# An attention and expert layer on one core: PSUM banks by name, and side work queued behind the score copies and adds

## The chip, the cores and the metric

The kernel runs on one core of one Trainium2 chip. The metric is the device time of an execution in microseconds (us), and of several executions the median. The time before is 2626.7 us (three runs, 2624.99 to 2631.52).

## The reference

The input x has 4096 rows (2 sequences of 2048) of 2048 numbers. Each row is normalised, and the normalised rows xn go through single-head attention with head width 512 and through a mixture of 64 small experts of rank 8; both results are added to x. All of it is fp32.

```
xn   = layernorm(x)
qkv  = xn @ Wqkv + bqkv            # q, k, v: 4096 x 512 each
attn = softmax(q k^T / sqrt(512))  # per sequence, 2048 x 2048
x   += (attn @ v) @ Wo + bo
gate = softmax over the 16 largest of 64 router scores, else 0
x   += ((xn @ A^T) * gate per group of 8) @ B^T * 2
```

## The kernel before

**Numbers and products.** TensorE multiplies in a rounded fp32 form. Each operand is split into a rounded part (ScalarE, `split_hi`, line 121) and the rest (VectorE, `split_lo`, line 124), and every product takes three matmuls (`PASSES`: rest x rounded, rounded x rest, rounded x rounded). The large products are also done on 2 x 2 block matrices with seven block products in place of eight. The seven steps are called P1 to P7, and they need sums of operands and sums of results.

**Stages.** From 0 to about 1321 us rows are normalised and projected: a first block of 512 rows (`first_block`), a second one, and then three pairs of blocks, each in seven phases P1, P2, P6, P5, P3, P7, P4 (`phase`). Side work (loads, splits, sums) is listed per phase in `beside` and dealt out between the pieces of a phase. From 1321 to 2015 us comes attention, then the output projection to the end.

**Attention.** Queries are taken in four pairs of 512-row blocks, `NPAIR` = 4, eight blocks in all. For each pair there are `NKS` = 8 key groups of seven score steps, 56 steps a pair, 224 in all. A score step (`score`) is six matmuls (line 1129) from a query operand `qt` and a key operand `kt`. Steps P1, P7, P2, P6, P4, P5, P3 follow each other, and P1 of the next group is put before P3. In a group, P1 and P2 add up in one PSUM bank, P7 and P4 in a second, and P6, P5, P3 in a third, called U, which first gets a copy of P1 (`seed`, line 1112, on ScalarE). Results leave as copies on ScalarE (lines 1142, 1144, 1147, 1155) or as adds on VectorE (lines 1149, 1152) into the score tiles `sp`, and running maxima M are kept (lines 1098, 1101).

When a block's scores are there, `maxes` reduces the maxima to one per query (a chain of small VectorE instructions that ends in `mq`, line 1176), and `spread` brings them to all partitions with one matmul (line 1186) and a ScalarE copy. `soft` subtracts them (line 1201), takes the exponential (line 1204), splits (tile `ph`) and adds up row sums L (lines 1212, 1214). `weigh` multiplies by the values: a block has 16 key tiles of four columns d of 128 output features, so 64 groups of three matmuls (line 129, tile `ph` by `vt`), which add up over the block in four banks `av`. Near the end of a block two matmuls (lines 1248, 1249) sum L over partitions, VectorE takes the reciprocal `rl` (line 1251), and after the last column the four divisions follow (line 1255), each with a bias on ScalarE (line 1256) and a store to DRAM (line 1257). The tiles `ot` have three buffers.

The value products of a pair run beside the scores of the next one, dealt evenly between `begin[i]` and `begin[i + 1]`. The last 9 of the 233 steps and the last pair have no scores beside them.

**Side work of attention.** The dictionary `side` holds steps by score number: key blocks split and stored for later pairs (`keys`: loads `kr`, casts and sums into `kst`, stores to `kp_d`), query operands (`query_load`, `query_split`), sums of queries (`query_steps`: four loads, four sums at lines 928 to 931, four stores, for each of two halves), and sums of output weights (`combos`).

**What sets the order.** A list scheduler orders the instructions of each engine when the kernel is built; each engine then runs its own queue in that order. `behind(keys)` adds an edge that keeps what is traced under it after a given instruction on the same engine. Under it, side steps of attention are kept behind the last key load on SyncE's queue:

```
for st in side.get(g, []):
    with behind("sp"):
        st()
```

[...] One, `misc`, is for small things. The other seven are one pool of seven buffers, from which the scheduler gives any free one:

```
def acc():
    return psum.tile([P, T], F32, name="acc", tag="acc", bufs=7)
```

Of the kernel before, what the change touches and what calls it, by code (L numbers as in the profile page):

```python
# [8 lines left out]
F32 = mybir.dt.float32  # L9
FR = mybir.dt.float32r  # L10
AF = mybir.ActivationFunctionType
# [5 lines left out]
P = 128  # L17
# [45 lines left out]
def attn_ffn_kernel(ctx: ExitStack, tc, x, xT, wq, wv, wob, bqk, bv, bo, keysT, out):  # L63
# [17 lines left out]
    def big(*js):  # L81
        return Ring(sb, *(f"B{j}" for j in js))
# [12 lines left out]
    for tag, words in order:  # L95
        sb.tile([P, words], F32, name=f"slot{tag}", tag=tag, bufs=1)

    def acc():
        return psum.tile([P, T], F32, name="acc", tag="acc", bufs=7)

    def misc(shape=None):
        return psum.tile(shape or [P, T], F32, name="misc", tag="misc", bufs=1)
# [49 lines left out]
    def oz_at(i, kind, c):  # L152
        return oz_d[i][c // 2, 2 * kind + c % 2]
# [507 lines left out]
    def beside(j, ph):  # L661
# [33 lines left out]
        if ph == "P3":  # L695
            if more:
                n = x_steps(j + 1, *b00)
                steps = mixed(split_steps(j, "P7", *b01), n[1][:2])
                return n[0], s1[-2:-1] + steps[:3] + s1[-1:] + steps[3:]
            return [], mixed(  # L700
                split_steps(j, "P7", *b01), query_steps(0, big(*GROUPS[3]), (0,))
            )
        if ph == "P7":
            if more:
                n = x_steps(j + 1, *b10)
                return n[0], mixed(split_steps(j, "P4", *b10), n[1][:2])
            ks_ = key_list(5, 7)
            return [], mixed(
                split_steps(j, "P4", *b10), query_steps(0, big(*GROUPS[3]), (1,)), ks_[:-4]
            ) + ks_[-4:]  # L710
        if more:
            return x_steps(j + 1, *b01)[0] + x_steps(j + 1, *b11)[0], mixed(
# [199 lines left out]
            steps += ops  # L912
        return steps

    def query_steps(j, ring, ds=(0, 1)):

        def steps(d):
            v = {}
            tt = nc.vector.tensor_tensor

            def load():
                for h in range(2):
                    for t in range(2):
                        v[h, t] = ring([P, T], F32, "qs")
                        nc.sync.dma_start(v[h, t], q_d[2 * j + t][h][:, d, :])

            def sums():
                tt(v[1, 1], v[1, 1], v[0, 1], ALU.subtract)
                tt(v[0, 1], v[0, 1], v[0, 0], ALU.subtract)
                tt(v[0, 0], v[1, 1], v[0, 0], ALU.add)  # L930
                tt(v[1, 0], v[1, 0], v[0, 0], ALU.subtract)

            def out():
                for k, at in enumerate(((0, 1), (0, 0), (1, 1), (1, 0))):
                    nc.sync.dma_start(qs_d[j][k][:, d, :], v[at])

            return [load, sums, out]

        return [st for d in ds for st in steps(d)]

    def query_load(j, n, ring=None):

# [163 lines left out]

    def seed(k):

        b = bank["U"] = acc()
        if k < 3:  # L1110
            nc.tensor.matmul(b, bank["k"], bank["q"], start=True, stop=True)
        nc.scalar.copy(b, bank["P1"])  # L1112

    def score(g):

# [5 lines left out]
            bank["U0"] = bank["U"]  # L1121
        name = {"P2": "P1", "P4": "P7", "P6": "U0", "P5": "U0", "P3": "U0"}.get(step, step)
        if not more:
            bank[step] = acc()
        ps = bank[name]
        st, mv = kop.pop(g), qop[j, step]
        for d in range(2):
            for i, (a, c) in enumerate(PASSES):
# [2 lines left out]
                    start=not more and d == 0 and i == 0, stop=d == 1 and i == 2,  # L1131
                    skip_group_check=more,
                )
        tt, copy = nc.vector.tensor_tensor, nc.scalar.copy
        if later:
            greatest(*later.pop())
        if step == "P1":
# [92 lines left out]
    def weigh(n):  # L1230

        c, d = divmod(n, ND)
        blk, k = blocks[c // NK], c % NK
        if d == 0:
            load_v(c + 3)
            soft(c + 2)
        if k == 0:
            av[blk, d] = acc()
        vt, ph = vt_[c], pt_[c]
        product(  # L1240
            av[blk, d], lambda a: vt[:, a, d * P : (d + 1) * P], lambda b: ph[:, b, :],
            k == 0, k == NK - 1,
        )
        if k == NK - 2 and d == 2:
            lh, ll = lsum[blk]
            with behind("pe"):
                pl = misc()
                nc.tensor.matmul(pl, onesr, ll, start=True, stop=False)
                nc.tensor.matmul(pl, onesr, lh, start=False, stop=True)
            rl_[blk] = r_rl([P, T], F32, "rl")  # L1250
            nc.vector.reciprocal(rl_[blk], pl)  # L1251
        if k == NK - 1 and d == ND - 1:
            for d in range(ND):
                ot = r_oo([P, T], F32, "ot")
                nc.vector.tensor_tensor(ot, av[blk, d], rl_[blk], ALU.mult)  # L1255
                nc.scalar.activation(ot, ot, AF.Identity, bias=bv_sb[:, d : d + 1])
                nc.sync.dma_start(oz_at(blk, 1, d), ot)

# [200 lines left out]
    NW = 2 * NK * ND  # L1461
    total = NPAIR * NG1

    begin = [NG1 * (j + 1) + (9 if j in (0, NPAIR - 1) else 5) for j in range(NPAIR)]
    side = {}

    def deal(g, steps, every=1):
# [18 lines left out]
        ks.update(R=mid(0, 1), st=mid(2, 3), n=1)  # L1486

    r_qs = wide(3, 4, 5, 9)
    for g, st in zip((2, 6, 8, 12, 16, 18), query_steps(1, r_qs)):
        deal(g, [st])  # L1490
    deal(NG1 + 2, [small_ring])
    for n, g in (
        (11, NG1 + 6), (12, NG1 + 18), (13, NG1 + 48), (14, 2 * NG1 + 9), (15, 2 * NG1 + 19)
# [23 lines left out]
    deal(begin[0] - 8, [lambda c=c: load_v(c) for c in range(3)])  # L1517
    deal(begin[0] - 3, [lambda c=c: soft(c) for c in range(2)])
    done = 0
    for g in range(begin[-1]):  # L1520
        if g < total:
            score(g)
# [1 line left out]
                key_load(g // 2 + 4)  # L1524
        j, n = divmod(g, NG1)
        for st in side.get(g, []):
            with behind("sp"):
                st()
        if j and j <= NPAIR:
            if n == 2:  # L1530
                maxes(2 * j - 1)
            if n in (1, 4):
                with behind("pe"):
                    spread(2 * j - 2 + n // 4)
        if n == NG1 - 2 and j < NPAIR:
            maxes(2 * j)
        for i in range(NPAIR - 1):
# [117 lines left out]
```

## Time and profile before

| | us |
|---|---|
| median of three runs (lowest, highest) | 2626.7 (2624.99, 2631.52) |
| profiled execution, its own time | 2629.96 |
| span of its instructions | 2628.2 |
| TensorE busy in matmuls | 2592.6 (99%) |
| VectorE busy | 1919.4 (73%) |
| ScalarE busy | 909.8 (35%) |
| GpSimd busy | 516.1 (20%) |

The profile is of one execution. An engine is busy while one of its instructions runs. Matmuls are pipelined and their ends are modelled, so a matmul has a mean of 389 ns though the next starts 227 ns after it. PE is TensorE's matmul side and PEld its weight loads, DVE is VectorE, ACT is ScalarE, POOL is GpSimd, SP is SyncE, whose queue issues nearly all DMAs. In a row of waits the columns are: the engine and line that waited, who released it, us in total, times, and the longest. In a row of a tile's instructions they are: least, median and largest ns, then first and last start. In a timeline row they are: start, us, engine, line, what it does, and in brackets the idle time before it and what ended that.

### The profile page before, as it was taken

Reading aid. Unit: us, or ns where it says so; the run is one execution under the profiler, and the core shown is the slowest. Engines: PE = TensorE matmul, PEld = TensorE weight load, DVE = VectorE, ACT = ScalarE, POOL = GpSimd, SP = SyncE. Lnnn points to the kernel's source line nnn. Section 1 sums busy time; section 2 is a strip of 40 time slices with the busy share of each in tenths; the row PEclk is TensorE's granted clock in tenths of the full one; section 3 lists DMA queues with packets and bytes.
Section 4 is the critical chain, followed back from the end, with each engine's and each line's share of the span. In section 5 each row is a group of like instructions: output and inputs, shape, how many; then the busy total and the mean of one; then the engine's idle time right before and its main releaser. Section 6 shows DMA issues by size and latency. Waiting matters only on the chain. (4 is left out here: it accounts for less than half of the span.)

```text
span 2628.2 us, 34501 instructions
## 1 busy us (share of the span) xinstructions
PE 2592.6 (99%) x12692; PEld 2186.3 (83%) x12692; DVE 1919.4 (73%) x2698; ACT 909.8 (35%) x1345; POOL 516.1 (20%) x315
## 2 busy tenths in 40 slices
PE   8999999999999999999989999999999999999999
PEld 7889888888888888888877877878888888888887
DVE  7557639867878677776758859678598776797675
ACT  4323223323332333343435436344364222332221
POOL 1311420000000000000000000000000765566654
PEclk9999999999999999999999999999999999999999
DMA  6667875668447683576999798799788544565542
GB/s 235 232 248 261 284 262 186 211 211 278 153 136 226 214 274 124 177 257 226 310 305 326 253 329 268 257 331 321 251 294 296 175 164 161 183 217 176 177 162 103
DMA packets 328954, 608.09 MB, mean 231 GB/s; under 512 B 27928, under 2 KB 150864, under 8 KB 328784
## 3 DMA queue, kind: packets, MB, share of 16 engines
q1 hardware_dynamic: 315824, 575.99, 64.9%
q10 hardware_dynamic: 12960, 29.89, 3.4%
q8 instruction: 100, 1.64, 0.3%
q14 instruction: 70, 0.57, 0.1%
HBM read 450.42 MB, written 155.35 MB: 230 GB/s over the span
## 5 line engine op out<-in xcount | busy, mean ns | idle before, releaser
L129 PE MATMUL acc<-t,pw 128*128 128x512 f32 x3024 | 694.0, 390 | 1.6 <-DVE pw L124 1.5
L129 PEld LDWEIGHTS acc<-t,pw 128*128 128x128 f32 x3024 | 565.3, 188 | 119.7 <-DVE pw L124 2.5
L1406 PE MATMUL acc<-wb,s 128*128 128x512 f32 x2688 | 609.4, 389 | 0.0
L1406 PEld LDWEIGHTS acc<-wb,s 128*128 128x128 f32 x2688 | 504.5, 188 | 104.8
L1390 POOL TENSOR_TENSOR xo<-xo,bo_bc 128x512 f32<-128x512 f32 x128 | 205.6, 1613 | 906.4 <-DMA vt<-v_d 606.2
L129 PE MATMUL acc<-ph,vt 128*128 128x512 f32 x1536 | 378.6, 391 | 4.5 <-DVE ot L1255 2.5
L1129 PE MATMUL acc<-qt,kt 128*128 128x512 f32 x1344 | 338.4, 394 | 14.3 <-ACT acc L1112 7.4
L129 PEld LDWEIGHTS acc<-ph,vt 128*128 128x128 f32 x1536 | 287.7, 188 | 68.5 <-DVE ot L1255 4.1
L1129 PEld LDWEIGHTS acc<-qt,kt 128*128 128x128 f32 x1344 | 253.1, 190 | 73.7 <-ACT acc L1112 8.3
L121 ACT CAST pw<-pw 128x1024 fp32r<-128x1024 f32 (+1 forms) x168 | 177.6, 1058 | 324.8 <-PE acc L129 240.9
L129 PE MATMUL acc<-xh,wh 128*128 128x512 f32 x1152 | 263.7, 390 | 0.0
L124 DVE TENSOR_TENSOR pw<-pw 128x1024 fp32r<-128x1024 f32 (+1 forms) x168 | 214.7, 1278 | 64.9 <-ACT pw L121 63.5
L129 PEld LDWEIGHTS acc<-xh,wh 128*128 128x128 f32 x1152 | 215.6, 188 | 44.9
L129 PEld LDWEIGHTS acc<-pw,t 128*128 128x128 f32 x2016 | 245.8, 188 | 1.3
L129 PE MATMUL acc<-pw,t 128*128 128x264 f32 x2016 | 246.4, 283 | 0.0
L121 ACT CAST s<-xz 128x1024 fp32r<-128x1024 f32 x112 | 118.0, 1054 | 368.7 <-PE acc L1406 285.8
L124 DVE TENSOR_TENSOR s<-xz,s 128x1024 fp32r<-128x1024 f32 x112 | 175.4, 1568 | 41.6 <-ACT s L121 41.6
L124 DVE TENSOR_TENSOR wh<-wu,wh 128x512 fp32r<-128x512 f32 x96 | 83.6, 888 | 99.0 <-ACT wh L121 99.0
L519 POOL TENSOR_TENSOR zt<-zt,g 128x512 f32<-128x512 f32 x24 | 38.9, 1630 | 503.3 <-DMA g<-gd 272.4
L121 ACT CAST t<-xq 128x1024 fp32r<-128x1024 f32 x84 | 88.3, 1052 | 103.5 <-PE acc L129 44.8
L124 DVE TENSOR_TENSOR t<-xq,t 128x1024 fp32r<-128x1024 f32 x84 | 108.2, 1292 | 20.6 <-ACT t L121 20.1
L1395 DVE TENSOR_TENSOR xo<-xo,acc 128x512 f32<-128x512 f32 x128 | 86.8, 679 | 49.1 <-PE acc L1406 22.3
(168 smaller groups left out, 2463.2 us busy)
## 6 DMA issues: line engine op xcount, KB each, us to landing
vt<-v_d SPq DMA_DIRECT2D x128, 512.0 KB, 5.3
kt<-kp_d SPq DMA_DIRECT2D x224, 256.0 KB, 5.8
pw<-sq_d SPq DMA_DIRECT2D x72, 512.0 KB, 4.0
xo<-in_x SPq DMA_DIRECT2D x128, 256.0 KB, 3.4
xz<-oz_d SPq DMA_DIRECT2D x64, 512.0 KB, 4.8
out_y<-xo SPq DMA_DIRECT2D x128, 256.0 KB, 2.3
pw<-in_wq SPq DMA_DIRECT2D x54, 512.0 KB, 4.4
wu<-in_wq SPq DMA_DIRECT2D x48, 512.0 KB, 5.9
```

Of the source, the lines that this page charges most:

```text
L121: return nc.scalar.copy(hi, src)
L124: return (eng or nc.vector).tensor_tensor(lo, src, raw(hi), ALU.subtract)
L129: last["pe"] = nc.tensor.matmul(ps, st(a_), mv(b_), start=first and n == 0, stop=end and n == 2)
L519: nc.gpsimd.tensor_tensor(zt, zt, gx[n], ALU.mult)
L1129: last["pe"] = nc.tensor.matmul(ps, st[:, d, a, :], mv[c][:, d, :], start=not more and d == 0 and i == 0, stop=d == 1 and i == 2, skip_gro ...
L1390: nc.gpsimd.tensor_tensor(xs, xs, bo_bc[q // (NB // 2 * NH), c], ALU.add)
L1395: nc.vector.tensor_tensor(xs, xs, ps, op)
L1406: nc.tensor.matmul(ps, st[a_][:, kk, sl], mv[b_], start=not more and kk == 0 and n == 0, stop=kk == ND - 1 and n == 2, skip_group_check=more,)
```

## The change

1. `acc()` gives banks by name, from 0 to 6. Without an argument the seven names go round. In attention the names are fixed: the four value columns have banks 0 to 3, P1/P2 has bank 4, U bank 5, P7/P4 bank 6. In the odd key groups of the first pair, when no value products run yet, P1, U and P7 have banks 0, 1 and 2.
2. A side step of attention is kept behind the last score copy on ScalarE and the last score add on VectorE too, besides the last key load.
3. The query sums of pair 1 leave attention for projection phase P7 of the last pair, and those of pair 0, which were half in P3 and half in P7, are all in P3.
4. The division of a column follows the last product of that column, not that of the fourth column.
5. The second maxima and both spreads come one score step later (steps 3, 2, 5 of a pair, not 2, 1, 4), and the value products of the middle pairs begin one step later.
6. One of three dummy matmuls in `seed` goes.

```diff
@@ -95,8 +95,14 @@
     for tag, words in order:
         sb.tile([P, words], F32, name=f"slot{tag}", tag=tag, bufs=1)
 
-    def acc():
-        return psum.tile([P, T], F32, name="acc", tag="acc", bufs=7)
+    banks = list(range(7))
+
+    def acc(n=None):
+
+        if n is None:
+            n = banks.pop(0)
+            banks.append(n)
+        return psum.tile([P, T], F32, name="acc", tag=f"acc{n}", bufs=1)
 
     def misc(shape=None):
         return psum.tile(shape or [P, T], F32, name="misc", tag="misc", bufs=1)
@@ -698,7 +704,7 @@
                 steps = mixed(split_steps(j, "P7", *b01), n[1][:2])
                 return n[0], s1[-2:-1] + steps[:3] + s1[-1:] + steps[3:]
             return [], mixed(
-                split_steps(j, "P7", *b01), query_steps(0, big(*GROUPS[3]), (0,))
+                split_steps(j, "P7", *b01), query_steps(0, big(*GROUPS[3]))
             )
         if ph == "P7":
             if more:
@@ -706,7 +712,7 @@
                 return n[0], mixed(split_steps(j, "P4", *b10), n[1][:2])
             ks_ = key_list(5, 7)
             return [], mixed(
-                split_steps(j, "P4", *b10), query_steps(0, big(*GROUPS[3]), (1,)), ks_[:-4]
+                split_steps(j, "P4", *b10), query_steps(1, big(*GROUPS[2])), ks_[:-4]
             ) + ks_[-4:]
         if more:
             return x_steps(j + 1, *b01)[0] + x_steps(j + 1, *b11)[0], mixed(
@@ -912,7 +918,7 @@
             steps += ops
         return steps
 
-    def query_steps(j, ring, ds=(0, 1)):
+    def query_steps(j, ring):
 
         def steps(d):
             v = {}
@@ -936,7 +942,7 @@
 
             return [load, sums, out]
 
-        return [st for d in ds for st in steps(d)]
+        return steps(0) + steps(1)
 
     def query_load(j, n, ring=None):
 
@@ -1106,10 +1112,10 @@
 
     def seed(k):
 
-        b = bank["U"] = acc()
-        if k < 3:
+        b = bank["U"] = acc(5 - 4 * (k < NKS and k % 2))
+        if k < 2:
             nc.tensor.matmul(b, bank["k"], bank["q"], start=True, stop=True)
-        nc.scalar.copy(b, bank["P1"])
+        last["copy"] = nc.scalar.copy(b, bank["P1"])
 
     def score(g):
 
@@ -1121,7 +1127,7 @@
             bank["U0"] = bank["U"]
         name = {"P2": "P1", "P4": "P7", "P6": "U0", "P5": "U0", "P3": "U0"}.get(step, step)
         if not more:
-            bank[step] = acc()
+            bank[step] = acc((4 if step == "P1" else 6) - 4 * (k < NKS and k % 2))
         ps = bank[name]
         st, mv = kop.pop(g), qop[j, step]
         for d in range(2):
@@ -1131,7 +1137,13 @@
                     start=not more and d == 0 and i == 0, stop=d == 1 and i == 2,
                     skip_group_check=more,
                 )
-        tt, copy = nc.vector.tensor_tensor, nc.scalar.copy
+
+        def tt(*ops):
+            last["add"] = nc.vector.tensor_tensor(*ops)
+
+        def copy(*ops):
+            last["copy"] = nc.scalar.copy(*ops)
+
         if later:
             greatest(*later.pop())
         if step == "P1":
@@ -1235,7 +1247,7 @@
             load_v(c + 3)
             soft(c + 2)
         if k == 0:
-            av[blk, d] = acc()
+            av[blk, d] = acc(d)
         vt, ph = vt_[c], pt_[c]
         product(
             av[blk, d], lambda a: vt[:, a, d * P : (d + 1) * P], lambda b: ph[:, b, :],
@@ -1249,12 +1261,11 @@
                 nc.tensor.matmul(pl, onesr, lh, start=False, stop=True)
             rl_[blk] = r_rl([P, T], F32, "rl")
             nc.vector.reciprocal(rl_[blk], pl)
-        if k == NK - 1 and d == ND - 1:
-            for d in range(ND):
-                ot = r_oo([P, T], F32, "ot")
-                nc.vector.tensor_tensor(ot, av[blk, d], rl_[blk], ALU.mult)
-                nc.scalar.activation(ot, ot, AF.Identity, bias=bv_sb[:, d : d + 1])
-                nc.sync.dma_start(oz_at(blk, 1, d), ot)
+        if k == NK - 1:
+            ot = r_oo([P, T], F32, "ot")
+            nc.vector.tensor_tensor(ot, av[blk, d], rl_[blk], ALU.mult)
+            nc.scalar.activation(ot, ot, AF.Identity, bias=bv_sb[:, d : d + 1])
+            nc.sync.dma_start(oz_at(blk, 1, d), ot)
 
 
 
@@ -1461,7 +1472,7 @@
     NW = 2 * NK * ND
     total = NPAIR * NG1
 
-    begin = [NG1 * (j + 1) + (9 if j in (0, NPAIR - 1) else 5) for j in range(NPAIR)]
+    begin = [NG1 * (j + 1) + (9 if j in (0, NPAIR - 1) else 6) for j in range(NPAIR)]
     side = {}
 
     def deal(g, steps, every=1):
@@ -1486,8 +1497,6 @@
         ks.update(R=mid(0, 1), st=mid(2, 3), n=1)
 
     r_qs = wide(3, 4, 5, 9)
-    for g, st in zip((2, 6, 8, 12, 16, 18), query_steps(1, r_qs)):
-        deal(g, [st])
     deal(NG1 + 2, [small_ring])
     for n, g in (
         (11, NG1 + 6), (12, NG1 + 18), (13, NG1 + 48), (14, 2 * NG1 + 9), (15, 2 * NG1 + 19)
@@ -1517,6 +1526,7 @@
     deal(begin[0] - 8, [lambda c=c: load_v(c) for c in range(3)])
     deal(begin[0] - 3, [lambda c=c: soft(c) for c in range(2)])
     done = 0
+    last["add"] = last["dve"]
     for g in range(begin[-1]):
         if g < total:
             score(g)
@@ -1524,14 +1534,14 @@
                 key_load(g // 2 + 4)
         j, n = divmod(g, NG1)
         for st in side.get(g, []):
-            with behind("sp"):
+            with behind("sp", "copy", "add"):
                 st()
         if j and j <= NPAIR:
-            if n == 2:
+            if n == 3:
                 maxes(2 * j - 1)
-            if n in (1, 4):
+            if n in (2, 5):
                 with behind("pe"):
-                    spread(2 * j - 2 + n // 4)
+                    spread(2 * j - 2 + n // 5)
         if n == NG1 - 2 and j < NPAIR:
             maxes(2 * j)
         for i in range(NPAIR - 1):
```

## The prediction

> **What bounds the kernel now.** I read the page's busy table first, then stretches by stage, then TensorE's waits in the attention stage, then the start times of single matmuls around each wait.
>
> ```profile
> PE 2592.6 (99%) x12692; PEld 2186.3 (83%) x12692; DVE 1919.4 (73%) x2698; ACT 909.8 (35%) x1345; POOL 516.1 (20%) x315
> L1406 PE MATMUL acc<-wb,s 128*128 128x512 f32 x2688 | 609.4, 389 | 0.0
> ```
> TensorE is the bound, with little to give: in the output projection 2688 matmuls take 609.4 us, 226.7 ns each, with no idle time. That is the floor for any 512-column matmul here.
>
> ```profile
> 0.00:1321.00 1321.00, 1310.07 (x7098) 1136.09 (x7099) 942.68 (x1476) 445.18 (x686) 146.74 (x91) 1.00 0.67 226
> 1321.00:2015.00 694.00, 673.24 (x2909) 545.99 (x2909) 534.11 (x802) 314.46 (x493) 9.94 (x7) 0.99 0.87 295
> 2015.00:2628.00 613.00, 609.32 (x2689) 504.20 (x2687) 442.56 (x421) 150.14 (x167) 359.40 (x217) 1.00 0.52 172
> ```
> After the stretch: its length, then busy us of PE, PEld, DVE, ACT, POOL, the clock and the DMA share. The attention stage, 694 us, holds some 2907 matmuls, at 226.7 ns 659 us: 35 us are lost. The busy column shows only 21 of them, because ends of matmuls are modelled. So only attention has something to win.
>
> ```profile
> PE acc L1129 <- ACT acc L1112: 7.4, 2, 7.2
> PE acc L1129 <- ACT sp L1155: 5.0, 5, 1.6
> PE acc L129 <- DVE ot L1255: 2.5, 2, 2.2
> PE acc L1129 <- DMA kt<-kp_d: 1.9, 3, 0.8
> PE misc L1186 <- DVE mq L1176: 1.8, 3, 1.0
> PE acc L129 <- DVE ph L124: 1.7, 2, 1.2
> ```
> Adding up, from the starts, what each interval has over 0.227 us, 33.9 us fall to: stage start 9.9, late score copies 7.4, maxima with their spreads (L1186) 5.4, key loads 3.1, block ends (division, softmax) 8.0. The start is ScalarE's queue:
>
> ```profile
> 1323.63 0.41 ACT L121 CAST kst<-kr 128x256 fp32r<-128x256 f32 x1 [9.56 <-DMA kr<-k_d]
> 1329.69 1.06 ACT L121 CAST vs<-vs 128x264 fp32r<-128x264 f32 x3 [0.32 <-DVE vs L289]
> 1330.65 0.57 ACT L1112 COPY acc<-acc 128x512 f32<-128x512 f32 x1
> ```
> Six casts of a key block, waiting for a load, stand ahead of the first seed copy, with the value casts behind them; the copy is all that TensorE lacks, and it stops from 1323.9 to 1331.3. At 1620.2 it is the same in small: key casts that wait for their stores stand ahead of an L1155 copy, and TensorE loses 1.8 us. The next 11 matmuls then start 0.427 us apart, not 0.227.
>
> ```profile
> L1251 DVE RECIPROCAL rl<-misc x8: 3339/3348/3358, 1500.9 to 2011.6; 128x512 f32<-128x512 f32 x8
> L1255 DVE TENSOR_TENSOR ot<-acc,rl x32: 671/678/693, 1505.9 to 2022.1; 128x512 f32<-128x512 f32 x32
> L1256 ACT ACTIVATE ot<-ot,bv_sb x32: 705/722/727, 1506.6 to 2022.8; 128x512 f32<-128x512 f32 x32
> DMA to landing us min/median/max: 2.2/3.5/6.0
> ```
> The chain at a block's end (the last line is its stores) matters below.
>
> [...] a stop of 2.4 us at 1511.6 was followed by 1.6 us of such loss and one of 2.4 us at 38.6 by none. [...] divisions at 1972.4 come only after the reciprocal of 1968.6 to 1971.9. [...] a new holder waits for the old one's reader, as at 1511.6 for the division.
>
> **The change part by part.** Where instructions land I take from the built order of each engine; counts are equal but for one dummy matmul less (-0.2 us).
>
> Side work behind copies and adds. The first seed copy now has three value casts ahead and no key cast; later, key casts alternate with copies. But the names put the first score in bank 4, held by the last value tile: two adds L289 (0.42 each) and hops, about 0.9 us, and some 0.3 for bank 6. Start: 9.9 becomes 1.2 (0.8 to 4). **-8.7.**
>
> Late copies. Before, P7 of the next key group took the bank that P3's copy (L1155) frees, one step earlier: six product matmuls, 1.36 us, to hide 0.59 plus the queue. Now P7 has bank 6, freed three steps before; P3's copy is wanted only by the next seed copy, and that by P2: 18 matmuls, 4.1 us, against 1.5 for both copies. The worst lateness seen (1.6 beyond 0.8) fits. 7.4 becomes 1.6 (0 to 5). **-5.8.** What the change pushes back, casts and sums for keys, queries and weights, is used steps later.
>
> Query sums. Pair 1's 8 sums (0.68 each), 8 loads and 8 stores (256 KB, 4.2 MB) leave 1321 to 1421, where the DMA share is 0.96. They go to phase P7 (1234 to 1278, share 0.83), and half of pair 0's from there to P3 (0.75). DVE is busy 33 and 28 of 44 us there, so 2.7 us more each are covered; 2.1 MB more in 44 us is 48 GB/s on 281, close to full. On SP they pass weight fetches, issued over a piece of 24 matmuls (5.4 us) ahead: +0.3 (0 to 3). Key loads: 3.1 becomes 1.6 (0 to 3). **-1.2.**
>
> Maxima later. One score step and its products, about 2.5 us, cover the worst mq wait (1.16); some 0.3 per spread stays, 8 times. 5.4 becomes 2.4 (2 to 4). **-3.0.**
>
> Division per column and named product banks. There are eight block ends; I number them 1 to 8, and the last three (6, 7, 8) come when all scores are done. A new block's column d now waits for the old one's division d; before, it could take any free bank, and without scores three were free. (At end 8 the next holder of bank 0 is the output projection's first sum.) From the second L1249 matmul to the end of the first division the trace has 6.1, 9.7, 5.3, 12.7, 7.4, 6.3, 7.1, 6.2 us (VectorE's queue over the bare 3.35 + 0.68). The new VectorE order adds a softmax cast and a maximum at ends 2 and 3 (1.2), takes about 2 from end 4, and a stop at end 6 lets VectorE gain about 1.8 for end 7: 6.1, 10.9, 6.6, 10.5, 7.4, 6.3, 5.3, 6.2. TensorE asks after 6.4, 8.1, 7.7, 9.0, 6.4 us (27 to 39 matmuls), but after 3.65 (15) at the three ends without scores: stops of 0, 2.8, 0, 1.5, 1.0, 2.6, 1.6, 2.5, together 12.0. The fourth division needs the first one's buffer back (0.72 + 3.5 + 0.68 and hops, 5.1 us) and TensorE comes after 17 matmuls (3.9) at end 6 and some 20 (4.5) at ends 1 and 2: 2.3. Half clock after the three long stops: 1.6 each, at even odds 2.4. Sum 16.7 (5 to 40) instead of 8.0: **+8.7.**
>
> First block. Naming puts the last transposes of row tile 1 into the bank of the first accumulator, so the statistics of tile 2 (2.46 us) start 2 us later; but TensorE waited 2.4 us anyway for those of tile 3, which come 0.4 later: **+0.4** (0 to 3). Projection and output order is otherwise the same.
>
> Sum: -8.7 - 5.8 - 1.2 - 3.0 + 8.7 + 0.4 - 0.2 = -9.8. The profiled execution took 2629.96 us (span 2628.2) and would take 2620.2; the median of the runs, 2626.7, is 3.3 lower: 2617.
>
> **The rivals.** (a) Slower: the ends decide. Where the reciprocal's chain is never absorbed, each of eight ends costs 3.5 us (the mean over the three without scores, with the fourth column) and 1.6 of half clock, 41 in all: 33 - 18.5 = +14.5, 2641. It needs over 26.5 us in all, 3.3 per end; 4.3 per end is 0.3%. For it: DVE is busy without a break from 1957 to 1975. Against: ends 1 and 3 have chains of 6.1 and 5.3 under TensorE's 6.4 and 7.7. (b) No change: copies stay late (5 of 7.4) and ends cost 21: 2625. For it: exponentials of 1.06 us still stand between P3's copy and the seed. (c) Everything hides: VectorE, relieved early, keeps ahead and ends cost 5: 2605. For it: the last reciprocal waited 1.8 us idle; against: nothing shortens 3.35.
>
> **How the numbers follow.** A measurement tells 0.3% (7.9 us) from no change. My forecast 0.40 and (c) 0.17 are faster; (b) and the weak side of my forecast 0.26; (a) 0.17. The range, 2603 to 2635, leaves about 0.1 out on each side; it takes in the bounds of the start, the copies and the loads, and most of (a).
>
> **What would show it.** Right: no key cast ahead of the first L1112; hardly any wait of L1129 on L1155; TensorE's longest stops at the last three block ends, on ot. Wrong: new waits on ACT or kt in the first pair, stops on pw near 1234 to 1278, or none at all at the ends.

## The result, and the profile after

The changed kernel takes **2638.36 us** (median of 20 runs, 2631.35 to 2643.02); beside it on the same chip the kernel before takes 2630.85 (20 runs). The ratio is 1.0029, 95% interval 1.0022 to 1.0036: **slower by 0.29%**, some 7.5 us. The forecast was 2617.0, the range ended at 2635. Of the 21 us between 2638 and 2617, 4 are the base: the forecast started from 2626.7, the median of three runs, and 20 runs have 2630.85. The profiled execution took 2636.47 us, its span is 2634.7; that of the kernel before had 2629.96 and 2628.2.

The busy times and the output projection's row, beside the two lines of the kernel before in the prediction:

```profile
PE 2594.2 (98%) x12691; PEld 2189.3 (83%) x12691; DVE 1917.2 (73%) x2698; ACT 911.1 (35%) x1345; POOL 519.3 (20%) x315
...
L1417 PE MATMUL acc<-wb,s 128*128 128x512 f32 x2688 | 609.6, 389 | 1.7 <-DVE ot L1266 1.7
```
One matmul fewer, and nothing else of the work has changed; the output projection still takes 609.6 us, but its first sum now waits 1.7 us for a division. The three stretches (length, then busy us of PE, PEld, DVE, ACT and POOL, the clock, the DMA share, GB/s), of the changed kernel:

```profile
0.00:1331.00 1331.00, 1313.29 (x7098) 1137.92 (x7098) 947.56 (x1487) 447.50 (x688) 150.16 (x91) 1.00 0.67 227
1331.00:2021.00 690.00, 671.36 (x2907) 546.79 (x2906) 530.43 (x794) 313.85 (x492) 10.82 (x7) 0.99 0.86 291
2021.00:2635.00 614.00, 609.57 (x2688) 504.60 (x2688) 439.22 (x419) 149.74 (x166) 358.32 (x217) 1.00 0.52 171
```
Attention, the only stage with something to win, went from 694 to 690 us, and what lies ahead of it from 1321 to 1331. So the forecast's place was right and its amount was not, and 10 us were lost where it had 0.7. By the starts of single matmuls: first two blocks 383.3 to 386.6, pairs 937.6 to 944.4, attention 694.0 to 690.3, output projection 609.4 to 609.6.

TensorE's waits in attention (what waits, for what; us in all, times, the longest) show what is gone and what is new:

```profile
PE acc L135 <- issue: 4.7, 2, 2.4
PE acc L135 <- DVE ot L1266: 3.8, 3, 2.2
PE acc L1135 <- ACT acc L1118: 2.6, 2, 1.7
PE misc L1198 <- DVE rl L1263: 1.9, 1, 1.9
PE acc L1417 <- DVE ot L1266: 1.7, 1, 1.7
PE acc L135 <- ACT ph L127: 1.6, 1, 1.6
```
The 7.2 us at the start are gone: no key cast stands ahead of the first seed copy any more, and no row is left in which TensorE waits for a score copy (`sp`, 5.0 us before). ScalarE's queue at the start:

```profile
1330.55 1.16 ACT L127 CAST vs<-vs 128x264 fp32r<-128x264 f32 x3 [2.54 <-DVE vs L295]
1332.80 0.57 ACT L1118 COPY acc<-acc 128x512 f32<-128x512 f32 x1 [1.09 <-PE acc L1117]
```
Five of the six rows are ends of blocks: columns that wait for a division, a spread that waits for the reciprocal. The rows "issue" and "ACT ph" hide the same cause. At the end near 1850 us the timeline of VectorE and TensorE has:

```profile
1845.68 3.35 DVE L1263 RECIPROCAL rl<-misc 128x512 f32<-128x512 f32 x1
...
1846.39 1.52 PE L135 MATMUL acc<-ph,vt 128*128 128x512 f32 x6
...
1849.49 1.88 DVE L1266 TENSOR_TENSOR ot<-acc,rl 128x512 f32<-128x512 f32 x3
...
1850.28 1.62 PE L135 MATMUL acc<-ph,vt 128*128 128x512 f32 x3 [2.36 <-issue]
```
The next block's first column starts 0.79 us after the start of the first division, which lasts 0.68: it waited for that division, and the division for the reciprocal. (At 1973.87, in the row "ACT ph", a column starts 0.77 us after the start of its division.) The three matmuls of the column take 1.62 us, not 0.84; that is half clock: the trace's clock records have a granted clock of 0.5 for 3.41 us from 1849.9 on, and matmuls start 0.427 us apart there.

At two ends, near 1596 and 1682 us, it is the fourth division that is late, and what it waits for is the store that frees its buffer `ot` (3.04 and 4.35 us):

```profile
1681.72 0.69 DVE L1266 TENSOR_TENSOR ot<-acc,rl 128x512 f32<-128x512 f32 x1 [4.35 <-DMA oz_d<-ot]
```

Ahead of attention there is one row of waits from 1200 to 1330 us, where the kernel before has none, and SyncE's queue says what stood in front:

```profile
PE acc L135 <- DVE pw L130: 4.9, 4, 2.0
```
```profile
1272.32 2.81 SPq L941 DMA_DIRECT2D qs_d<-qs  x4
1275.19 0.42 SPq L873 DMA_DIRECT2D kp_d<-kst  x1
1275.66 1.45 SPq L612 DMA_DIRECT2D pw<-in_wq  x2
```
L941 are stores of the moved query sums; the weight fetches L612 are issued behind them, and TensorE stops at 1281.6 for 2.0 us on the split of such a weight. The fetch at 1275.66 comes some 6 us before TensorE needs it; in the kernel before the same fetch was issued at 1254.8 and needed at 1276.7, 22 us later. The fetches of this stretch take about as long to land as before (median 5.8 and 5.6 us). So they come late because they are issued late.

### The profile page after: what moved, and what is told of

It is laid out like the page before. It is cut to its first block, busy times and chain, and to the rows that moved or that the text cites. A ratio compares the mean times of both kernels' runs of the same rounds, so it can differ in the third digit from the quotient of the medians.

```text
span 2634.7 us, 34458 instructions
## 1 busy us (share of the span) xinstructions
PE 2594.2 (98%) x12691; PEld 2189.3 (83%) x12691; DVE 1917.2 (73%) x2698; ACT 911.1 (35%) x1345; POOL 519.3 (20%) x315
## 4 chain that ended last, share of the span: by engine, by line
PE 88%; DMA 6%; DVE 4%; issue 1%; ACT 1%; SPq 0%; POOL 0%; DVEq 0%; ACTq 0%
PE acc L135 54%; PE acc L1417 23%; PE acc L1135 9%; DMA pw<-in_wq 1%; DMA oz_d<-ot 1%; DMA kt<-kp_d 0%; DMA vt<-v_d 0%; DMA qs_d<-qs 0%; DMA kr<-k_d 0%; DMA kp_d<-kst 0%; DVE rl L1263 0%; DVE sp L1213 0%; DVE qt L130 0%; PE misc L403 0%; ACT pw L127 0%
## 5 line engine op out<-in xcount | busy, mean ns | idle before, releaser
L1417 PE MATMUL acc<-wb,s 128*128 128x512 f32 x2688 | 609.6, 389 | 1.7 <-DVE ot L1266 1.7
```

The lines of the kernel that those rows point to most:

```text
L1417: nc.tensor.matmul(ps, st[a_][:, kk, sl], mv[b_], start=not more and kk == 0 and n == 0, stop=kk == ND - 1 and n == 2, skip_group_check=more,)
```

## The experiments

Fourteen kernels, in four groups, each compared with the kernel before on the same chip. That kernel's median lay between 2627.3 and 2631.4 us from group to group, so ratios are compared and not times. Stages are of one profiled execution each (us), and the last column counts half clock in stretches of 3.4 us, in attention and the stop before its first score: the kernel before has 10.24 and 3.41 us of it, counted as 4, the changed kernel three times 3.41. Stages of single executions scatter: a_names and the changed kernel have attention's instructions in the same order on TensorE and VectorE, and take 696.1 and 690.3 us for it, with the same stops in other sizes; p_earlymax and p_earlymaxrl have the same pairs, and take 936.6 and 940.1. A difference of less than 6 us in one stage shows little by itself.

| kernel | ratio to before (95%) | first blocks | pairs | attention | half clock |
|---|---|---|---|---|---|
| before | 1 | 383.3 | 937.6 | 694.0 | 4 |
| changed | 1.0029 (1.0022 to 1.0036) | 386.6 | 944.4 | 690.3 | 3 |
| a_names | 1.0042 (1.0029 to 1.0054) | 386.3 | 943.3 | 696.1 | 3 |
| a_qback | 1.0034 (1.0021 to 1.0046) | 386.0 | 940.9 | 695.7 | 5 |
| a_pool | 0.9989 (0.9979 to 0.9999) | 382.8 | 946.2 | 676.0 | 0 |
| b_side | 0.9989 (0.9978 to 0.9999) | 386.9 | 938.1 | 686.0 | 1 |
| p_qpool | 0.9980 (0.9971 to 0.9989) | 383.2 | 941.9 | 677.6 | 2 |
| p_qback | 0.9984 (0.9977 to 0.9991) | 386.4 | 937.9 | 687.4 | 3 |
| p_div | 0.9996 (0.9987 to 1.0005) | 384.6 | 946.7 | 677.6 | 1 |
| p_max | 0.9978 (0.9969 to 0.9987) | 384.9 | 945.2 | 678.8 | 1 |
| a_rl | 0.9987 (0.9979 to 0.9995) | 386.1 | 946.8 | 683.1 | 1 |
| a_div | 1.0024 (1.0016 to 1.0031) | 386.4 | 945.2 | 693.8 | 4 |
| p_early | 0.9956 (0.9944 to 0.9968) | 384.5 | 941.5 | 677.5 | 0 |
| p_earlymax | 0.9948 (0.9934 to 0.9961) | 384.5 | 936.6 | 675.4 | 0 |
| b_names | 1.0031 (1.0020 to 1.0042) | 386.7 | 945.7 | 692.7 | 5 |
| p_earlymaxrl | 0.9943 (0.9929 to 0.9958) | 386.8 | 940.1 | 678.0 | 1 |

**a_names: the projections' banks as before.**
```
+    order_of = [0, 6, 5, 4, ...]     # 252 banks
     def acc(n=None):
+        if n is None and order_of:
+            n = order_of.pop(0)
         if n is None:
```


> The changed kernel with one thing undone: the first 252 accumulators of the projections get the banks, by name, that the pool of seven gave them in the kernel before; the last fourteen, attention and the output projection keep the changed names. My theory now: the rotation of names costs the first two blocks 3.2 us (383.34 before, 386.55 changed), because the last transposes of the second row tile fall into the first accumulator's bank and hold back the statistics of the third tile; the 6.8 us that the pairs lost come from SyncE's queue. Then the first two blocks end at 383.3 +- 0.7, the pairs stay at 944 +- 2 long, and the whole takes 3 us less than the changed kernel, 2635 +- 2, about 4 to 5 over the kernel before. Rival 1 (names cost the pairs too): both stages go back, the pairs to 938, and the whole takes 10 us less, 2628, a little under the kernel before. Rival 2 (the first block's 3 us are the spread between executions): 386 stays, and the whole is 2638.

Measured: 1.0042, no gain. The time lost in the first 50 us of the trace falls from 12.2 us to 10.6 (before: 10.2), so 1.6 to 2.0 us of it are the names'. But the first blocks still end at 386.3, with two stretches of half clock in their first 60 us; b_side, whose projections are those of the kernel before, ends them at 386.9 with three. The theory held for 2 us in the trace, not for the whole; the rest of the 3.2 us goes with where half clock fell.

**a_qback: query sums back in attention.**
```
-split_steps(j, "P4", *b10), query_steps(1, big(*GROUPS[2])), ...
+split_steps(j, "P4", *b10), query_steps(0, big(*GROUPS[3]), (1,)), ...
+for g, st in zip((2, 6, 8, 12, 16, 18), query_steps(1, r_qs)):
+    deal(g, [st])
```


> The changed kernel with the query sums of the second pair back in attention and those of the first back over two projection steps, as in the kernel before; everything else is as changed. My theory: in the last steps of the pairs SyncE issues the stores of the query sums, four of 2.8 us each, ahead of weight fetches that TensorE then waits for (1.1, 2.0, 1.4 and 0.95 us at 1268.8, 1281.6, 1305.5 and 1324.2). Then the pairs fall from 944.4 to 939 +- 1.5, attention keeps its start within 2 us since its side work is queued behind the copies and adds, and the whole takes 4 to 5 us less than the changed kernel: 2634 +- 2. Rival 1 (the waits for weights come from the names, or from the keys' stores, which stay): the pairs stay at 944 and the whole changes by less than 1.5. Rival 2 (what left the pairs comes back in attention, as the 9.9 us of stops at its start did in the kernel before): the pairs gain 5, attention loses 5 or more, and the whole is at 2638 to 2643.

Measured: all stops late in the pairs are gone, 944.4 to 940.9, and the whole is no faster: 1.0034 against 1.0029. That is rival 2's direction. Attention has 695.7 us where the changed kernel has 690.3, but a_names has 696.1 with the sums away from it, so that this profile alone doesn't show where the gain went.

**a_pool: one pool of seven.**
```
 def acc(n=None):
-    ...
-    return psum.tile([P, T], F32, name="acc", tag=f"acc{n}", bufs=1)
+    return psum.tile([P, T], F32, name="acc", tag="acc", bufs=7)
```
(The seed's dummy matmul is there for a third unit again.)

> The changed kernel with every accumulator drawn from one pool of seven again (so attention's too), and all the rest as changed. My theory: the first two blocks go back to 383.3 +- 0.7; the pairs keep 944 +- 2; in attention the late score copies return in part (4.1 us of stops now, 7.4 in the kernel before), while a block's first column may take any free bank, so the ends cost less than the 18.4 us now, by 2 to 6. Whole: 2634 +- 3, 2 to 7 less than the changed kernel. Rival 1 (the names carry the gain of attention's start, since its first matmul no longer waits for a bank): the start loses its 8.7 us again and the whole is at 2643. Rival 2 (the names are the whole loss): 2626, under the kernel before.

Measured: 2624.23 us, 0.40% less than the changed kernel by the ratios, 10.5 us; rival 2 was nearest. TensorE's waits in attention, whole list but one row of 0.2:

```profile
PE acc L1129 <- ACT sp L1139: 4.0, 3, 2.2
PE acc L1129 <- DVE ot L1260: 2.0, 1, 2.0
PE misc L1192 <- DVE rl L1257: 1.3, 1, 1.3
PE misc L1192 <- DVE mq L1182: 1.1, 1, 1.1
PE acc L129 <- DVE ot L1260: 1.1, 1, 1.1
```
Attention takes 676.0 us and not 690.3. Of these 14.3, some 4.8 are three stretches of half clock (3.41 us each, 1.6 of them lost) that the one pool does not have, and 9.5 are stops. By the starts of the matmuls the block ends, half clock included, cost 3.6 us here and about 18 with names: that is nearly the whole difference. The pairs keep their loss (946.2): that isn't the names'. Attention's start did not get worse without names. Late copies did, a little: the waits for score copies are back (L1139, 4.0), where the named kernel waits 2.6 for the seed copy L1118.

**b_side: the side work's queueing alone, in the kernel before.**
```
-with behind("sp"):
+with behind("sp", "copy", "add"):
     st()
```


> The kernel before with one part of the change alone: attention's side work is queued behind the last score copy and the last add too, and not behind the last weight fetch alone. Nothing else is changed: pool of seven, query sums in attention, division at the block's end, maxima early. My theory: the stops at attention's start, 9.9 us in the kernel before, 1.2 in the changed one, fall by 6 to 9; first blocks and pairs stay at 383.3 and 937.6; block ends stay at 8 +- 4. Whole: 2622 +- 3, 6 to 9 less than the kernel before, and faster than both. Rival 1 (the start was mended by taking the second pair's query sums out of attention, not by the queueing): under 2 us of gain, 2629. Rival 2 (the side work now comes late and holds up the keys or the next pair's queries): over 2632.

Measured: attention begins without a stop, where it had 7.4 us and 2.5 of half clock after it; its first, 1.6 us, comes 17 us later. Attention is 8.0 us shorter. So the queueing mends the start by itself. It does not mend the late score copies, for which TensorE still waits 5.7 us. The whole gained only 0.11% (2.9 us, interval 0.3 to 5.8): less than half of the 6 to 9 expected, so that the trace speaks against rival 1 and the runs don't settle it.

**p_qpool: the query sums' transfers on POOL's queue.** All p_ kernels have one pool of seven.
```
-nc.sync.dma_start(qs_d[j][k][:, d, :], v[at])
+(nc.gpsimd if j < 2 else nc.sync).dma_start(qs_d[j][k][:, d, :], v[at])
```
The loads likewise.

> The kernel with the whole change but one pool of seven (the run with all accumulators from one pool, 2624.2), and in it the loads and stores of the query sums that lie in the projections are issued on POOL's queue; the later ones stay on SyncE's. My theory: SyncE's queue is what TensorE's waits for weights in the last two steps of the pairs come from (5.4 us of stops between 880 and 940 us of the stage). Then these stops go, the pairs fall from 946.2 to 940 +- 1.5, attention stays at 676 +- 4, and the whole takes 4 to 6 us less, 2619 +- 3: faster than both kernels. Rival 1 (VectorE's or ScalarE's own order delays the splits, as the sums themselves are in VectorE's queue): no change in the pairs, 2624. Rival 2 (the transfers from POOL's queue cost its engine time that other work needs, or land late for attention's query loads): attention's start loses 3 or more, 2624 to 2628.

Measured: no wait for pw is left after 1200 us, but another has come, on a split of activations:

```profile
PE acc L129 <- DVE t L124: 2.6, 2, 1.8
PE acc L129 <- ACT t L121: 0.5, 1, 0.5
```
VectorE had stood still for 3.9 us at 1278.4, until a store of keys landed. The pairs fall by 4.3, the whole by 0.09%, inside the intervals. So SyncE's queue made the waits for weights; the first such fetch is issued at 1258.2 here, 19 us before it is needed. Whether the new wait comes of the crowd of transfers or of the key store's place in a queue isn't shown.

**p_qback: query sums back, with one pool.** The edit of a_qback.

> As the run with one pool of seven, with the query sums back as in the kernel before (second pair's in attention). My theory: the pairs fall from 946.2 to 940 +- 1.5; attention's start takes the sums with stops of 1 to 5 us, as in the run with query sums back and named banks (5.1 us of stops in its first 100 us, 3.6 in the changed kernel). Whole: 2624.2 - 6 + 3, 2621 +- 3. Rival (what left the pairs all comes back in attention): 2624 to 2626.

Measured: 0.9984 against 0.9989, no difference. The pairs win 8.3 and attention loses 11.4: 5 us of stops in its first 120 us, the rest in later stops, with three stretches of half clock; the seven other kernels with the changed side work, one pool and the sums in the projections have attention at 675 to 679. **Moving the query sums between these two places shifts a loss and removes none**; the rival was right.

**p_div: divisions at the block's end.**
```
-if k == NK - 1:
-    ot = r_oo([P, T], F32, "ot")
+if k == NK - 1 and d == ND - 1:
+    for d in range(ND):
+        ot = r_oo([P, T], F32, "ot")
```


> As the run with one pool of seven, with the four divisions of a block all issued after its last product again. My theory: the division per column is worth little by itself once a block's first column may take a bank that a score has freed: the ends cost 1 to 3 us more, since the banks come free up to 2 us later and the next scores take them. Attention 676 to 679, whole 2625 +- 3. Rival 1 (the division per column is where attention's gain over the kernel with the side work alone, 686 to 676, comes from): attention 684 or more, whole 2632. Rival 2 (the early divisions hold up the adds on VectorE): attention shorter by 2 or more, whole 2621.

Measured: attention 677.6, the whole 0.07% (2 us) up, inside the intervals of 2 to 3 us on either side. With one pool the division per column isn't told apart from nothing.

**p_max: maxima, spreads and weighing early again.**
```
-    begin = [NG1 * (j + 1) + (9 if j in (0, NPAIR - 1) else 6) for j in range(NPAIR)]
+    begin = [NG1 * (j + 1) + (9 if j in (0, NPAIR - 1) else 5) for j in range(NPAIR)]
-            if n == 3:
+            if n == 2:
                 maxes(2 * j - 1)
-            if n in (2, 5):
+            if n in (1, 4):
```


> As the run with one pool of seven, with the maxima, spreads and the beginning of the weighing one step earlier again, as in the kernel before. My theory: the spread of a block's maxima no longer falls behind the row sums and their reciprocal in the one bank that both use (that wait, 1.3 us, goes), but waits for its maxima (3.0 us in the kernel before with the side work alone, 1.1 in the run with one pool): attention 677 to 680, whole 2626 +- 3. Rival 1 (the later start of the weighing, six steps in place of five, is what gives the block's end room for the reciprocal and the divisions): attention 684 or more, whole 2632. Rival 2: attention shorter by 1 or more, 2622.

Measured: 0.9978 against 0.9989, not slower: the later maxima bring nothing. The spread's waits for mq are 3.0 us here against 1.1 in a_pool, and the 1.3 for rl are gone, as expected; the whole does not follow. This wait for rl stands in each of the ten profiles with late maxima (0.3 to 2.8 us) and in none of the six with early ones.

**a_rl: the reciprocal two products earlier, with names.**
```
-if k == NK - 2 and d == 2:
+if k == NK - 2 and d == 0:
     lh, ll = lsum[blk]
```


> The changed kernel (named banks) with one thing moved: the row sums' matmuls and the reciprocal of a block are issued two products earlier, at the first column of its second-last tile in place of the third. My theory: with named banks a block's first column must wait for the division of the block before, and so for the reciprocal, since no bank is spare. With the reciprocal some 1.4 us or more earlier, the stops of 2.4 to 2.5 us at block ends (348.9, 516.6, 593.1 us of attention) fall under 1.2 each, the half clock that follows two of them (1.6 us each) goes, and so does the spread's wait behind the reciprocal (2.0 us, with half clock 3.9): 8 +- 3 us less, 2630 +- 3. Rival 1 (VectorE's own queue, not the reciprocal's place in it, sets the division): the stops stay and the whole is 2637. Rival 2 (the row sums now wait for the last exponentials' splits and stop TensorE themselves): new waits of 1 us or more at the row sums, 2636 to 2640.

Measured: 2627.89 us, ratio 0.9987 where the changed kernel has 1.0029: this line takes back 11 us, as much as giving up the names. TensorE's waits in attention begin:

```profile
PE misc L1198 <- DVE mq L1188: 4.3, 2, 3.3
PE acc L1135 <- ACT acc L1118: 2.4, 3, 1.7
PE acc L135 <- DMA vt<-v_d: 1.7, 2, 1.5
PE acc L1417 <- DVE ot L1266: 1.5, 1, 1.5
PE acc L135 <- DVE ot L1266: 1.4, 1, 1.4
```
The "issue" row fell from 4.7 to 0.5, ot from 3.8 to 1.4, the spread's wait for rl from 1.9 to 0.3; a wait for mq of 3.3 is new. The fourth division's waits for a store shrink too, from 2.3 to 4.4 us at four ends to at most 1.6. With names, the reciprocal's chain is what most of the block ends' time hangs on. A fourth `ot` buffer was not tried.

**a_div: divisions at the block's end, with names.** The edit of p_div, in the changed kernel.

> The changed kernel (named banks) with the four divisions of a block issued after its last product again. My theory: with named banks the division per column is needed, as each next column waits for its own bank; moved back, the first column's division starts up to 2 us later and each block end costs 1 to 2 us more: attention 690 + 7 to 14, whole 2645 +- 4. Rival (the divisions wait for the reciprocal anyway, which ends after the last product, so that their place in the program counts for nothing): within 2 us of the changed kernel, 2637.

Measured: 1.0024 against 1.0029, and my theory falls: the rival was right. The waits for ot are 5.5 and not 3.8, but the divisions come after the reciprocal wherever they stand in the program.

**p_early and p_earlymax: query sums earlier still; the second with the maxima early too.** (Excerpts; the phase stands in front.)
```
 P2: mixed(..., split_steps(j, "P6", *b00), queries(0, 0))
 P6: mixed(*steps, queries(0, 1), ...)    P5: ... queries(1, 0)    P3: ... queries(1, 1)
+r_qe = Ring(sb, "B25", "B26", "H6", "H7")
```


> As the run with one pool of seven, with the query sums made earlier: the four loads, four sums and four stores of each of the four parts lie beside one projection step of the last pair each (P2, P6, P5, P3, that is 1000 to 1240 us), in buffers that are free there, in place of all sixteen in P3 and P7. DMA engines are 65 to 79% busy at 1100 to 1250 us and 90 to 92% from 1250 on in the run with one pool. My theory: what the pairs lost is transfers crowded into the last 80 us, not the sums' own cost. Then the pairs fall from 946.2 to 938 +- 1.5 and attention stays at 676 to 679: 2617 +- 3, the fastest so far. Rival 1 (the stores pass weight fetches on SyncE wherever they lie): waits for weights of 1 to 2 us each appear in these four steps, and the whole is 2622 to 2625. Rival 2: attention loses what the pairs gain, 2624.

> The run just named with the maxima, spreads and the beginning of the weighing one step earlier as in the kernel before. My theory: the two changes are independent, and the maxima's place is worth 0 to 2 us either way (2624.2 with them late, 2622.5 with them early, in runs whose intervals overlap): 2616 +- 4. Rival (they are worth 3 us or more for the early place, because the spread never meets the reciprocal): 2613 or less.

Measured: 0.9956 and 0.9948, under both kernels. From 1200 us to attention, p_early has one wait for a weight:

```profile
PE acc L129 <- DVE pw L124: 0.5, 1, 0.5
```
The pairs take 941.5 (2.5 of it one wait 182 us into the stage, far from the sums) and 936.6 us, and attention keeps its 675 to 678. So the query sums' gain in attention is real and their cost in the pairs was their place. The DMA share from 1250 us on stays at 0.91, as in a_pool: it isn't the share that makes the stops. The first weight fetch of the stretch is issued at 1259.6, 21 us before TensorE needs it, about as in the kernel before. The rival of p_earlymax (3 us or more for the early maxima) isn't shown: the ratios differ by 2 us, and the two intervals overlap.

**b_names: names alone, in the kernel before.** The bank numbers of acc, seed, score and the weighing, and the one dummy matmul less.

> The kernel before with the names of the accumulators alone: the rotation of seven in the projections and the output projection, and fixed banks in attention, as the change has them. Everything else is as before. My theory: names alone take from the kernel before about what they took from the other parts of the change (2638 with names against 2624 with one pool): the block ends get stops of 2 to 3 us where a first column waits for the division, while attention's start keeps its stops or part of them. 10 to 16 us more than the kernel before: ratio 1.004 to 1.006. Rival (the names are bad only together with the later start of the weighing, or with the division per column): within 3 us of the kernel before, ratio under 1.0015.

Measured: 1.0031, 8 us: a little under what was expected, well over the rival. The names cost about as much without the other parts as with them. They do take away the waits for score copies (5.0 us before, 0.2 here), but they don't mend the start:

```profile
PE acc L1135 <- DVE vs L295: 6.8, 1, 6.8
```
The first score waits as long as in the kernel before, now for adds L295 that free its bank (this stop stands in the pairs' column of the table).

**p_earlymaxrl: the earlier reciprocal, with one pool.** The edit of a_rl in p_earlymax.

> The fastest run so far (one pool of seven, query sums early, maxima early; ratio 0.9948 to the kernel before) with the row sums and the reciprocal two products earlier. My theory: the 10 us that the earlier reciprocal saved with named banks (2638 to 2628) came from first columns that had no spare bank; with one pool a first column takes a bank that a score has freed, so that the same edit is worth no more than 2 us either way: ratio 0.994 to 0.9955. Rival (the reciprocal is late in every version, and ends at blocks profit the same): 5 us or more less, ratio 0.993 or under. Rival 2 (the early row sums now meet the spread in the one bank that both use): 3 us or more slower, 0.996 or over.

Measured: 0.9943 against 0.9948, within the 2 us of the theory. The line that is worth 11 us with names is worth next to nothing without, so it is the missing spare bank that makes the reciprocal's time count. (This kernel differs from a_rl in the maxima and the query sums too.) In both kernels the earlier reciprocal brings a longer wait for mq, 3.3 and 3.1 us at the longest, against 0.5 and 0.9 without it. This kernel, 2614.8 us, is the fastest by its median; against p_earlymax it isn't told apart.

## Why the prediction was wrong

By its own profile the change cost 6.5 us where the sum had -9.8: 16.3 apart. The largest part is the query sums' term for the projections, 6.5; then come the maxima, 5.1, the first blocks, 2.8, and the late copies, 2.5.

- **Query sums, -1.2: the step that failed most.** The term "+0.3 (0 to 3)" for the projections measured 5.4 us of stops (1.1, 2.0, 1.4 and 0.8, all on weight splits), over its bound. The prediction had named the cause, sums that pass weight fetches on SyncE, and let 5.4 us of lead cover it. But landing (5.8 us) and the splits (1.05 and 1.22) need 8, and the kernel before had given 22; with the sums ahead the lead fell to 6. On the other side attention's gain was missed as well: with one pool it lost 11.4 us, half clock included, when the sums went back. Both sizes were off, and the net, nothing, came near -1.2 by luck.
- **Maxima later, -3.0: wrong in sign.** 5.4 us became 7.5 in the profile; in the runs, with one pool, the late maxima bring nothing. Spread and row sums share the one `misc` bank, and one step later the spread came behind the row sums: at 1584 it waited 1.9 us for the reciprocal, and 3.41 us of half clock followed. "Some 0.3 per spread" took no account of the bank's other user.
- **Start of attention, -8.7: right in the profile.** 9.9 became 1.0, and that is a wait for a key load and not for the bank. The first seed copy (L1118) has three value casts in front of it and no key cast; b_side has the gain alone, b_names has it not. The runs of b_side show only 2.9 us for the whole.
- **Late score copies, -5.8: the reason right, the size half.** By the starts, 7.4 became 4.1. The names were to do it, and they did: waits for score copies are 0 to 0.2 us in the six kernels with names and 2.8 to 5.7 in the ten with one pool, the kernel before among them. But 0.9 to 3.0 us of waits for the seed copy came in their place. At 1423.5 that copy stands behind an exponential of 1.06 us, as rival (b) had said.
- **Block ends, +8.7: the size nearly right, its reading wrong.** 8.0 became about 18 where 16.7 were forecast; 1.4 of it is a load of values. At ends 6, 7 and 8 the stops are where they were put (2.5, 1.8, 1.9 us; forecast 2.6, 1.6, 2.5). Elsewhere the end-by-end list was poor: ends 3 and 5, forecast 0 and 1.0, have 2.4 (the fourth division waited 4.35 for its buffer's store) and 2.5, each with 3.41 us of half clock, and ends 2 and 4, forecast 2.8 and 1.5, 0.8 and nothing. So the total owes something to luck. And the prediction treated the ends as a fair price for what the names gain at the copies. a_pool and b_names show that it is not: names cost 8 to 11 us net, since with one pool the ends come down to 3.6. Rival (a), "the ends decide", was nearest with 2641, though they came to 18 and not 41 us.
- **First blocks, +0.4: too small.** 3.2 in the profiles; 1.6 to 2.0 of it are stops where the named bank holds back the statistics, within the given 0 to 3. The rest goes with half clock: 3.41 us from 20.4 on, where the kernel before has none in these blocks.

One reading of the trace was wrong too: the 11 matmuls 0.427 us apart follow the stop at the start, at 1331.3. After the stop at 1620.2 matmuls start 0.227 apart.

What the terms come to: attention -3.6 in place of -10.5, pairs +6.8 in place of +0.3, first blocks +3.2 in place of +0.4. Measured part by part from the ratios: side work -2.9 us, names +8 to +11, query sums, division and maxima together nothing. These add up to the 7.5 measured within their intervals; the prediction's terms for the same parts were -8.7, +3.3 (copies, ends, first blocks) and -4.2.

Open is why b_side won 8.0 us in attention in its profile and 2.9 in its runs, and what part of the ends the store of `ot` makes.

## What to carry to other kernels

A pool keeps a spare buffer where names fix who waits for whom: before naming banks, ask at each handover what the old holder's last reader itself waits for (here a 3.35 us reciprocal), and move that earlier first. Before moving side work to where an engine has slack, look at the queue that it shares with the stream that the bound engine lives on, and spread it thin: sixteen loads and sixteen stores in two steps cost 5 us, the same over four steps, three of them earlier, nearly nothing. A bank shared by two users makes a moved instruction meet the other one.

## What the runs showed of the hardware

Half clock is a granted clock of 0.5 in a trace's clock records. The changed kernel has it three times in attention, from 1587.1, 1682.6 and 1849.9 us, for 3.41 us each. Matmuls of 512 columns start 0.427 us apart there and not 0.227, so that 3.41 us hold seven or eight starts in place of fifteen: 1.6 us are lost. The sixteen profiles have 0 to 5 such stretches in and just before attention (last column of the table), so half clock is a part of the scatter between them.

Each of the three came with a stop of TensorE: 2.0 us at 1584.3, 2.4 at 1679.8 and 2.5 at 1847.5. But the same trace has stops of 2.0 us at 1281.6 and of 2.5 at 1924.1 with no half clock after them. The kernel before shows both cases too: 2.4 us at 1511.6 with 3.41 us of half clock from 1514.0 on, and 2.4 us at 38.6 with none; in its stop of 7.4 us at 1323.7 half clock begins at 1326.2 and lasts 10.24 us, 5 of them after the stop. So in these two traces a stop of 2.0 to 2.5 us cost 1.6 us more or nothing. What decides between the two was not shown. For this kernel it means that a forecast should count such a stop at its own length and up to 1.6 us more, as the prediction did at even odds.
